# Banded distances: from differences and squares to products of queries parted on a grid

## The chip, the cores and the metric

The kernel runs on one core of one Trainium2 chip. The metric is the device time of one launch in microseconds. The core has five engines that work side by side and wait for each other by semaphores: TensorE (PE in the profile, its weight loads PEld), VectorE (DVE), ScalarE (ACT), GpSimd (POOL) and SyncE (SP), whose queue issues nearly all DMAs here. Data lies in SBUF and PSUM (128 partitions each) and in DRAM.

## The reference

Four layers run over x of shape (8, 1024, 128), each added to its input after a layer norm: full attention (16 heads), a feed-forward layer with weights of plus and minus one (called F1 below), a banded "top 32 of 64" attention, and the same feed-forward layer again (F2). The change touches only the banded attention:

```
q = relu(x @ encoder_query);  v = relu(x @ encoder_value)       # 8 heads of 16
metric = softplus(base_metric + 0.1 * mod)                      # from the mean of q, per batch, head, column
idx = clip(pos[:, None] - arange(64)[None, :], 0, T - 1)        # each row and the 63 before it
for h in range(8):
    diff = q_h[:, idx] - q_h[:, :, None]
    dist = sqrt((diff * diff * metric_h).sum(-1) + 1e-08)
    top 32 of 64 by smallest dist
    infl = exp(-topd) / (sum + 1e-08)
    context = sum(infl * v_h[rows chosen]) + gate * 0.1 * (qhat @ Hm)
    outs.append(q_h * context)
x = x + stack(outs) @ decoder
```

## The kernel before, in words

`full_attention` runs first over all eight batches and takes about half of the time. The other three layers follow together in `mixed_stages`. There each batch is described by generators of small operations, and a planner (`Issue`, from L63) merges all of them into one order before anything is issued. Each operation names its engine with an assumed length, what it needs and gives, and the buffers ("rings") that it takes and drops. The planner repeatedly takes the operation that can start earliest, the one due first among equals. It so sets the order on every engine and on SP's queue; at run time each engine goes through its own list in order and waits where it must. The assumed lengths, such as 2.6 for DVE's selection of a head pair, 0.2 for SP's two band stores and 2.5 for a DMA's landing, set the order only.

For each batch the steps are:

- `front` normalises x, turns it, projects the queries into `qT` (128 columns of all heads on the partitions, 1024 positions and a pad of 64 copies of the first) and computes the metric (DVE operations up to L1288, ACT's L1270).
- `differences` (L1330): for each half of 512 positions and each of 16 groups of four offsets, one operation subtracts the queries from the queries four times shifted, 128 x 2048 elements. Of the 32 such operations of a batch most go to POOL and three to DVE; in the first half of batch 0 the planner may use either (39 on DVE and 217 on POOL in all). The result, `sq`, has four buffers.
- `squares` (L1345) squares each of them on ACT; `distances` (L1362) multiplies by minus the metric and sums the 16 columns of each head on PE; `turned` (L1380, L1390, L1403) copies, transposes and copies, which gives `nd`, the negative squared distances with positions on the partitions: 128 positions x 4 tiles x 8 heads x 64 offsets for one half.
- `picks` (L1443, L1446) on DVE: for each tile of 128 positions and each head four rounds of "eight largest, then mark them". One planner operation does two heads; four make a tile, 64 tiles in all.
- `influence` (L1418) takes the root of a half; `selection` takes exp (L1466), keeps the chosen (L1478), sums (L1480) and divides (L1496) into `wr`. Two DMAs on SP write `wr` as bands into a DRAM buffer `skew` whose rows are shifted by one against each other (L1509); one DMA reads the buffer back straight, as `wb` (L1515). So a band becomes a 128 x 128 matrix per head.
- `contexts`: PE projects the values (L1599), transposes `wb` into `pw` (L1619), ACT copies it (`wT`, L1630), PE weighs the values (`pc`, L1646), DVE multiplies by the queries (`c`, L1659), PE decodes (`pd`, L1668) and DVE adds to x (L1673). `scaled` prepares the gated queries `qg`.
- The feed-forward units of F1 and F2 (L1023 to L1154) fill in between: POOL normalises, PE multiplies (L1070, L1105, L1132), ACT and DVE apply relu and split (`xh` L1059, `h` L1090), DVE adds (L1148).

`wb` has two buffers, `wT` one, `nd` three; a context therefore follows its tile's selection by some steps on every engine. What sets the end of a band is the way `wr` - `skew` - `wb` - `pw` - `wT` - `pc` - `c`.

Of the kernel before, what the change touches and what calls it, by code (L numbers as in the profile page):

```python
# [12 lines left out]
F32 = mybir.dt.float32  # L13
# [8 lines left out]
P = 128  # L22
# [31 lines left out]
SQ_BUFS = 4  # L54
# [8 lines left out]
class Issue:  # L63
# [24 lines left out]
    def next_slot(self, name):  # L88

        count, slots = self.rings[name]  # L90
        if name != self.ANY:
            return slots[count % len(slots)], count % len(slots)
        return min([(t, i) for i, t in enumerate(slots) if t is not None], default=(None, None))

    def begin(self, op):
# [6 lines left out]
        for name, _ in op.takes:  # L102
            t = self.next_slot(name)[0]
            if t is None:
                return []
            at = max(at, t + self.HOP)
# [180 lines left out]
def hybrid_kernel(ctx: ExitStack, tc: tile.TileContext, a: dict, out: bass.AP):  # L287
# [6 lines left out]
    ps_acc = ps_one = ident = None  # L294
# [14 lines left out]
    def load(pool, key, shape, view=None):  # L309
# [13 lines left out]
        "mn_b2": [P, 1], "base": [P, 1], "dec": [P, P], "nblk": [P, 4, SLOT], "pblk": [P, NH], "hm": [P, P],  # L323
# [8 lines left out]
    for t in range(NT):  # L332
        skew.append(dskew.tile([P, NH * P], F32, tag=f"skew{t}", name=f"skew{t}"))

# [601 lines left out]
    def mixed_stages():  # L936
        nonlocal ps_acc, ps_one
        with ExitStack() as st:
            ps_acc = st.enter_context(tc.tile_pool(name="ps_acc", bufs=2, space=PSUM))
            ps_one = st.enter_context(tc.tile_pool(name="ps_one", bufs=1, space=PSUM))  # L940
            def one(name):
                return bank(name, issue.slot)
            dlast = st.enter_context(tc.tile_pool(name="d_last", bufs=1, space=DRAM))
            pools = {
                n: st.enter_context(tc.tile_pool(name=f"mx{n}", bufs=n)) for n in (1, 2, 3, SQ_BUFS, 8)
# [3 lines left out]
            enc_q, enc_v, mn_w1, mn_b1, mn_w2, mn_b2, base, dec, nblk, pblk, hm = (  # L949
# [4 lines left out]
            for v in values:  # L954
                V.memset(v, 0.0)
            issue = Issue()
            for name, n in (
                ("acc", 2), ("one", 6), ("sq", SQ_BUFS), ("qT", 3), ("xnT", 3), ("qg", 2),
                ("nd", 3), ("e", 1), ("wk", 2), ("wr", 2), ("wb", 2), ("wT", 1), ("qv", 2), ("c", 2), ("nt", 2), ("gx", 1),
                ("fxn", 1), ("wxn", 1), ("xh", 2), ("h1", 1), ("h2", 1), ("statsQ", 2), ("statsF2", 2),  # L960
            ):
                issue.ring(name, n)
# [198 lines left out]
            def front(b, f):  # L1161
# [132 lines left out]
                def columns(e):  # L1294
                    f["mst"] = tile_(2, [P, 4, SLOT], "mst", f"mst_{b}")
                    A.activation(f["mst"], nblk, AF.Copy, scale=f["met"])

                yield op([("A", 0.35)], columns, needs=[(k, "met")], gives=[(k, "metric")])


            FOURS = [(blk, kk) for blk in range(4) for kk in range(4)]


            BESIDE = (0,), (0, 2)

            def differences(b, f):

                for half in range(2):
                    for n, (blk, kk) in enumerate(FOURS):
                        k = ("now", b, half)  # L1310
                        if n == BESIDE[half][0]:
                            def now(e, half=half):
                                f["now"] = one(f"now_{b}_{half}")
                                A.copy(f["now"], f["qT"][:, WIN + half * 512 : WIN + half * 512 + 512])

                            yield op([("A", 0.58)], now, needs=[(("Q", b), "qT")], gives=[k], takes=[("one", k)])

                        beside = n in BESIDE[half]
                        lanes = [("V", 2.35)] if beside else [("L", 2.35)] if b == 0 and half == 0 else [("G", 4.2)]

                        def go(e, half=half, blk=blk, kk=kk, beside=beside):
                            f["sq", half, blk, kk] = tile_(SQ_BUFS, [P, 4, 512], "sq", f"sq_{b}_{half}_{blk}_{kk}")
                            now = f["qT"][:, WIN + half * 512 : WIN + half * 512 + 512]
                            back = bass.AP(
                                now.tensor, now.offset - (16 * blk + kk + 12), [now.ap[0], [4, 4], [1, 512]]
                            )
                            if beside and e != "G":
                                now = f["now"]
                            lane = G if e == "G" else V
                            lane.tensor_tensor(  # L1330
                                f["sq", half, blk, kk], back, now.unsqueeze(1).to_broadcast([P, 4, 512]), ALU.subtract
                            )

                        yield op(
                            lanes, go, needs=[k if beside else (("Q", b), "qT")],
                            gives=[("d", b, half, blk, kk)], takes=[("sq", (b, half, blk, kk))],
                            drops=[("one", k)] if n == BESIDE[half][-1] else (),
                        )

            def squares(b, f):  # L1340
                for half in range(2):
                    for q in FOURS:
                        def go(e, key=("sq", half) + q):
                            s = f[key].rearrange("p a q -> p (a q)")
                            A.activation(s, s, AF.Square)  # L1345

                        yield op(
                            [("A", 1.95)], go, needs=[("d", b, half) + q], gives=[("s", b, half) + q]
                        )

            def distances(b, f):

                for half in range(2):
                    for blk in range(4):
                        for kk in range(4):
                            q = (half, blk, kk)

                            def go(e, half=half, blk=blk, kk=kk, q=q):
                                if kk == 0:
                                    f["psd"] = ps_acc.tile([P, 512], F32, tag="acc", name=f"psd_{b}_{half}_{blk}")  # L1360
                                for cg in range(4):
                                    PE.matmul(  # L1362
                                        f["psd"][cg * SLOT : (cg + 1) * SLOT, :], f["mst"][:, kk, :],
                                        f[("sq",) + q][:, 3 - cg, :], start=(kk == 0), stop=(kk == 3),
                                    )
                                f["psd", half, blk] = f["psd"]

                            yield op(
                                [("T", 1.05)], go, needs=[("s", b) + q, (("Q", b), "metric")],
                                gives=[("psd", b, half, blk)] if kk == 3 else (),  # L1370
                                takes=[("acc", (b, half, blk))] if kk == 0 else (), drops=[("sq", (b,) + q)],
                            )

            def turned(b, f):

                for half in range(2):
                    for blk in range(4):
                        def copy(e, half=half, blk=blk):
                            f["nt", half, blk] = tile_(2, [P, 512], "nt", f"nt_{b}_{half}_{blk}")
                            A.copy(f["nt", half, blk], f["psd", half, blk])  # L1380

                        yield op(
                            [("A", 0.58)], copy, needs=[("psd", b, half, blk)], gives=[("nt", b, half, blk)],
                            takes=[("nt", (b, half, blk))], drops=[("acc", (b, half, blk))],
                        )

                        def turn(e, half=half, blk=blk):
                            f["pt"] = one(f"pt_{b}_{half}_{blk}")
                            for i in range(4):
                                PE.transpose(  # L1390
                                    f["pt"][:, i * P : (i + 1) * P], f["nt", half, blk][:, i * P : (i + 1) * P], ident
                                )

                        yield op(
                            [("T", 0.6)], turn, needs=[("nt", b, half, blk)], gives=[("pt", b, half, blk)],
                            takes=[("one", ("pt", b, half, blk))] + ([("nd", (b, half))] if blk == 0 else []),
                            drops=[("nt", (b, half, blk))],
                        )

                        def put(e, half=half, blk=blk):  # L1400
                            if blk == 0:
                                f["nd", half] = tile_(3, [P, 4, NH, WIN], "nd", f"nd_{b}_{half}")
# [454 lines left out]
```

## Time and profile before

| what | value |
|---|---|
| median of 3 runs | 2678.91 us (2676.65 to 2679.77) |
| profiled execution, span | 2688.0 us |
| PE busy, whole span | 2449.8 us, 22084 matmul records |
| DVE busy | 2360.5 us, 8495 instructions |
| ACT busy | 2110.5 us, 2764 |
| POOL busy | 1361.2 us, 962 |
| DMA moved | 116.69 MB, mean 43 GB/s; queue of SP 19.2% of 16 DMA engines |
| HBM | 45.79 MB read, 27.26 MB written |
| first MAX8 of a selection starts | 1523.4 us |

The span runs from the first to the last instruction of one profiled execution and is 9.1 us above the median of the timed runs. Busy time of an engine counts a moment once, however many of its instructions overlap; instructions of DVE and PE are pipelined, so their single durations overlap by about a tenth of a microsecond and the sum of a group's durations is more than the time it takes. The mean of a group hides different shapes, so groups are taken by form.

### The profile page before, as it was taken

The page shows a single profiled execution, that of the slowest core. Times are in us where ns is not written, and L with a number is a line of the kernel's source. Part 1 is how long each engine was busy: PE and PEld are TensorE (multiplying, and loading weights), DVE is VectorE, ACT ScalarE, POOL GpSimd, SP SyncE. Part 2 cuts the span into 40 slices and gives each one's busy share as a digit, 9 for nine tenths or more (in the row PEclk, how much of TensorE's full clock was granted, in tenths as well). Part 3 has the DMA queues.
Part 4 walks back from the last instruction along what each step waited for, and adds up shares of the span by engine and source line. Part 5 has one row for each costly group of instructions (what it writes and reads, how often), then busy time and mean ns, then how long its engine had stood idle before and what let it go on. Part 6 is the DMA issues. An engine that isn't in the chain of part 4 may idle for free.

```text
span 2688.0 us, 59925 instructions
## 1 busy us (share of the span) xinstructions
PE 2449.8 (91%) x22084; PEld 1387.5 (52%) x22084; DVE 2360.5 (88%) x8495; ACT 2110.5 (79%) x2764; POOL 1361.2 (51%) x962
## 2 busy tenths in 40 slices
PE   5999999999999999999999786998988898989677
PEld 2444444444444444444448363665656575746266
DVE  6999899898998989989954989999889999998985
ACT  1888788887888878888884878888888888888752
POOL 3202404114041140410203589999998999999931
PEclk6999999999999999999999888999989999989797
DMA  3312232121221212122100021222111222122221
GB/s 76 71 30 58 48 72 48 24 51 23 42 41 32 45 28 42 37 37 41 34 8 11 1 48 48 50 54 49 46 37 50 50 54 50 41 52 48 56 56 44
DMA packets 149693, 116.69 MB, mean 43 GB/s; under 512 B 96984, under 2 KB 127640, under 8 KB 149400
## 3 DMA queue, kind: packets, MB, share of 16 engines
q1 hardware_dynamic: 146216, 111.75, 19.2%
q8 instruction: 174, 2.85, 0.5%
q10 hardware_dynamic: 3184, 1.12, 0.2%
q14 instruction: 119, 0.97, 0.1%
HBM read 45.79 MB, written 27.26 MB: 27 GB/s over the span
## 4 chain that ended last, share of the span: by engine, by line
PE 62%; DVE 12%; POOL 10%; ACT 8%; DMA 5%; issue 2%; SPq 0%; ACTq 0%; POOLq 0%; DVEq 0%
PE acc L741 19%; PE ps L708 15%; PE pm L659 11%; POOL sq L1330 8%; DVE wk L1446 4%; PE psd L1362 3%; DVE m L1443 3%; ACT sq L1345 2%; DMA wb<-skew 2%; DMA skew<-wr 2%; DVE mx L663 1%; ACT e L720 1%; PE pw L1619 1%; PE pp L512 1%; POOL wxn L1023 1%
## 5 line engine op out<-in xcount | busy, mean ns | idle before, releaser
L663 DVE TENSOR_REDUCE mx<-pm 128x2 f32<-128x1024 f32 x1024 | 1202.3, 1217 | 137.2 <-PE pm L659 130.5
L1330 POOL TENSOR_TENSOR sq<-qT 128x2048 f32<-128x2048 f32 x217 | 896.4, 4162 | 7.8 <-PE psd L1362 7.5
L720 ACT ACTIVATE e<-ps 128x1024 f32<-128x1024 f32 x671 | 687.5, 1025 | 174.3 <-PE ps L708 153.4
L708 PE MATMUL ps<-q,k 64*128 64x512 f32 x2048 | 580.7, 443 | 13.2 <-ACT e L727 7.3
L741 PE MATMUL acc<-e,v 128*32 128x256 f32 x8192 | 591.1, 389 | 0.0
L1345 ACT ACTIVATE sq<-sq 128x2048 f32<-128x2048 f32 x256 | 488.4, 1916 | 50.6 <-POOL sq L1330 43.0
L659 PE MATMUL pm<-k,q 64*128 64x512 f32 x2048 | 490.3, 450 | 17.6 <-DMA q<-qs 9.0
L683 POOL TENSOR_TENSOR negm<-mm,negm 128x16 fp32r<-128x16 f32 x64 | 14.9, 233 | 818.9 <-ACT negm L682 818.9
L727 ACT ACTIVATE e<-ps 128x512 f32<-128x512 f32 x706 | 419.3, 594 | 5.0 <-PE ps L708 4.9
L708 PEld LDWEIGHTS ps<-q,k 64*128 64x128 f32 x2048 | 256.5, 185 | 262.5 <-ACT e L720 146.7
L1362 PE MATMUL psd<-sq,mst 128*32 128x512 f32 x2048 | 294.1, 653 | 75.5 <-ACT sq L1345 73.2
L741 PEld LDWEIGHTS acc<-e,v 128*32 128x32 f32 x8192 | 195.0, 109 | 289.5 <-issue 213.7
L659 PEld LDWEIGHTS pm<-k,q 64*128 64x128 f32 x2048 | 215.2, 187 | 188.8 <-DVE mx L663 85.4
L1446 DVE MATCH_REPLACE8 wk<-m,wk 128x64 f32<-128x64 f32 x1536 | 309.9, 210 | 0.0
L1443 DVE MAX8 m<-wk 128x8 f32<-128x64 f32 x1536 | 267.2, 217 | 0.0
L1619 PE MATMUL pw<-ident,wb 128*128 128x128 f32 x512 | 90.0, 309 | 56.8 <-DMA wb<-skew 49.3
L1446 DVE MATCH_VALUE_LOAD wk<-m,wk 128x8 f32 x1536 | 125.0, 81 | 0.0
L1619 PEld LDWEIGHTS pw<-ident,wb 128*128 128x128 f32 x512 | 65.8, 157 | 100.4 <-issue 53.6
L1362 PEld LDWEIGHTS psd<-sq,mst 128*32 128x32 f32 x2048 | 42.8, 111 | 135.5 <-ACT sq L1345 105.9
L1630 ACT COPY wT<-pw 128x512 f32<-128x512 f32 x128 | 74.2, 585 | 48.5 <-PE pw L1619 48.3
L1446 DVE MATCH_REPLACE8 wk<-m,nd 128x64 f32<-128x64 f32 x512 | 103.3, 210 | 0.0
L1443 DVE MAX8 m<-nd 128x8 f32<-128x64 f32 x512 | 87.5, 213 | 10.9 <-ACT nd L1403 10.9
(2211 smaller groups left out, 3739.8 us busy)
## 6 DMA issues: line engine op xcount, KB each, us to landing
wb<-skew SPq DMA_DIRECT2D x64, 512.0 KB
k<-ks SPq DMA_DIRECT2D x256, 64.0 KB
skew<-wr SPq DMA_DIRECT2D x128, 128.0 KB
q<-qs SPq DMA_DIRECT2D x252, 64.0 KB
x<-in_x SPq DMA_DIRECT2D x8, 512.0 KB
q<-dm SPq DMA_DIRECT2D x256, 8.0 KB
skew<-zeros SPq DMA_DIRECT2D x8, 512.0 KB
out_x<-x SPq DMA_DIRECT2D x32, 128.0 KB
```

What stands on the lines that cost most here:

```text
L659: PE.matmul(ps[:, j * 512 : j * 512 + 512], q[r, t * P : (t + 1) * P], k[r, kh * 512 : kh * 512 + 512], start=True, stop=True,)
L663: V.tensor_reduce(D["mx", n][:, kh, t, 2 * pair : 2 * pair + 2], ps.rearrange("p (j k) -> p j k", j=2), AX.X, ALU.max, negate=True,)
L708: PE.matmul(ps, sides[n % 3]["k", pair][r, c * P : (c + 1) * P], sides[n % 3]["q", pair][r, half * 512 : half * 512 + 512], start=True, st ...
L720: A.activation(e, ps, AF.Exp, scale=SCALE)
L727: A.activation(es[u], ps, AF.Exp, scale=SCALE)
L741: PE.matmul(acc[h * SLOT : (h + 1) * SLOT, part * 256 : part * 256 + 256], v[:, c, (g * 4 + h) * (HD_A + 1) : (g * 4 + h) * (HD_A + 1) + S ...
L1330: lane.tensor_tensor(f["sq", half, blk, kk], back, now.unsqueeze(1).to_broadcast([P, 4, 512]), ALU.subtract)
L1345: A.activation(s, s, AF.Square)
L1362: PE.matmul(f["psd"][cg * SLOT : (cg + 1) * SLOT, :], f["mst"][:, kk, :], f[("sq",) + q][:, 3 - cg, :], start=(kk == 0), stop=(kk == 3),)
L1443: V.max(m8, wk_[:, h, :] if n else f["nd", half][:, t % 4, h, :])
L1446: V.match_replace(out=wk_[:, h, :], in_to_replace=m8, in_values=wk_[:, h, :] if n else f["nd", half][:, t % 4, h, :], imm_value=SELECTED,)
L1619: PE.transpose(g["pw", hh][:, i * P : (i + 1) * P], f["wb", t][:, hh * 4 + i, :], ident)
```

## The change

The squared distance is computed as a product instead of by subtraction. With p = q times the square root of the metric, -d2/2 between a query row i and a key row j is p_i.p_j - |p_i|2/2 - |p_j|2/2. Here p is parted into h, rounded on a coarse grid (by adding and subtracting a large number `big`), and l = p - h, and the products of the parts are summed. Each head then has 52 rows: for the queries h, h, l and the norms, for the keys h, l, p and the norms, with rows of ones against the norms.

What happens now for each batch, besides the old steps that stay:

- `front` loses `columns` and gains `weighed`, `bound`, `roots` and `refined`: the bound `big` (a small product on PE and a root on ACT) and the root of the metric, refined by one step on DVE.
- `rows` for each half (512 positions and the 64 before them): ACT rounds (`h`), POOL scales (`p`) and takes off the bound, ACT squares `h`, POOL forms `l`, p + h and (p + h) l; three DMAs store `h`, `p`, `l` (each 128 x 576) in DRAM; twelve DMAs fetch them, sixteen rows at a time, into `queries` and `keys` (two heads of a pair on partitions 0 and 64, four pairs beside each other); PE sums the norms, ACT copies them, one DMA stores and four fetch them.
- `grams` for each tile: 16 products of 52 rows, 64 queries by 128 keys, into two PSUM banks, one product in each quarter of the array; two ACT copies, with the columns in reverse, into `dt`; one DMA stores the tile in `flat`; two DMAs fetch the bands from rows shifted by one, straight into `nd`; POOL clamps at zero.
- `picks` of a tile wait for that tile's band only, no longer for the half. `nd` has two buffers in place of three; the sums `acc` give their two PSUM banks to the common ring, which has eight. The heads stand in another order in `nd`, which `weigh` follows.
- The scratch space for DMAs issued by POOL is set to 1024.

Deleted: `differences`, `squares`, `distances`, `turned` and the constant `nblk`. Full attention is unchanged.

```diff
-                def columns(e):
-                    f["mst"] = tile_(2, [P, 4, SLOT], "mst", f"mst_{b}")
-                    A.activation(f["mst"], nblk, AF.Copy, scale=f["met"])
...
+                def weighed(e):
+                    f["mw"] = tile_(2, [P, 1], "mw", f"mw_{b}")
+                    V.tensor_scalar(f["mw"], f["met"], squared[0], None, ALU.mult)
...
+                    PE.matmul(f["psb"][:, 0:1], blk, f["mw"], start=True, stop=True)
...
+                    A.activation(f["root"], f["met"], AF.Sqrt)
+                    A.activation(f["big"], f["psb"][:, 0:1], AF.Sqrt, scale=GRID)
...
+                    V.tensor_scalar(f["sm"], f["root"], 1e-18, None, ALU.max)
+                    V.reciprocal(f["sm"], f["sm"])
+                    V.tensor_scalar(f["sm"], f["sm"], f["met"], f["root"], ALU.mult, ALU.add)
+                    V.tensor_scalar(f["sm"], f["sm"], 0.5, None, ALU.mult)
...
+            ROWS = ((0, "h", 2), (0, "h", 18), (1, "h", 2), (1, "p", 34), (0, "l", 34), (1, "l", 18))
+            NORMS = ((0, 1), (50, 51))
+
+            def rows(b, f):
...
+                        A.activation(g["h"], q(), AF.Identity, bias=f["big"], scale=f["sm"])
...
+                        G.tensor_scalar(g["p"], q(), f["sm"], None, ALU.mult)
+                        G.tensor_scalar(g["h"], g["h"], f["big"], None, ALU.subtract)
...
+                        [("A", 0.7)], lambda e, g=g: A.activation(g["2"], g["h"], AF.Square), needs=[(k, "h")],
...
+                        [("G", 1.25)], lambda e, g=g: G.tensor_tensor(g["l"], g["p"], g["h"], ALU.subtract),
...
+                        [("G", 1.25)], lambda e, g=g: G.tensor_tensor(g["w"], g["p"], g["h"], ALU.add),
...
+                        [("G", 1.25)], lambda e, g=g: G.tensor_tensor(g["w"], g["w"], g["l"], ALU.mult),
...
+                        S.dma_start(parted[half][name], g[name])
...
+                    def send(e, side, name, at, half=half):
+                        to, skip = ((queries, WIN), (keys, 0))[side]
+                        src = parted[half][name].rearrange("(g a d) t -> a d g t", g=NH // 2, a=2)
+                        for par in range(2):
+                            r = par * 64 + at
+                            S.dma_start(to[half][r : r + HD, :, :], src[par, :, :, skip:])
...
+            def grams(b, f):
...
+                        for g in range(NH // 2):
+                            for par, a2 in ((0, 0), (1, 1), (0, 1), (1, 0)):
+                                r = slice(par * 64, par * 64 + 52)
+                                c = c0 + a2 * 64
+                                PE.matmul(
+                                    ps[par][a2 * 64 : a2 * 64 + 64, g * P : (g + 1) * P],
+                                    queries[half][r, g, c : c + 64], keys[half][r, g, c : c + P], start=True, stop=True,
+                                )
...
+                            v = f["dt", t][:, par * 4 : par * 4 + 4, P - 1 : P]
+                            A.copy(
+                                bass.AP(v.tensor, v.offset, [list(v.ap[0]), list(v.ap[1]), [-1, P]]),
+                                f["pg", t][par].rearrange("p (g c) -> p g c", c=P),
                             )
...
+                    def store(e, t=t):
+                        S.dma_start(flat[t].rearrange("p (h c) -> p h c", c=P), f["dt", t])
...
+                            band = bass.AP(
+                                s.tensor, s.offset + a2 * 64 * NH * P + WIN - 1,
+                                [[NH * P - 1, 64], [P, NH], [1, WIN]],
                             )
...
+                            S.dma_start(f["nd", half][a2 * 64 : a2 * 64 + 64, t % 4], band)
...
+                        G.tensor_scalar(v, v, 0.0, None, ALU.min)
...
-                            AF.Sqrt, bias=tiny_t, scale=-1.0,
+                            AF.Sqrt, bias=tiny_t, scale=-2.0,
...
-                        [("V", 2.6)], marks(hh), needs=[("nd", b, half)],
+                        [("V", 2.6)], marks(hh), needs=[("nd", b, t)],
...
-                    ("differences", differences, 0.0, 1.0),
-                    ("squares", squares, 0.0, 1.0), ("distances", distances, 0.0, 1.0), ("turned", turned, 0.1, 1.05),
+                    ("rows", rows, -0.15, 0.35), ("grams", grams, 0.1, 1.0),
...
-    nc = bacc.Bacc("TRN2", target_bir_lowering=False, num_devices=1)
+    nc = bacc.Bacc("TRN2", target_bir_lowering=False, num_devices=1, dynamic_dma_scratch_size=1024)
```

## The prediction

> **What bounds the kernel now.** I read the page's forty slices first, to place the change, then busy time by window, the costliest groups, the waits, and the timelines of DVE and SP.
>
> ```profile
> DVE  6999899898998989989954989999889999998985
> POOL 3202404114041140410203589999998999999931
> ...
> 1406.00:2688.00 1282.00, 1086.07 (x9541) 751.44 (x9537) 1130.40 (x7300) 987.49 (x1212) 1042.90 (x524) 0.92 0.18 45
> 1469.00:1523.00 54.00, 43.20 (x320) 24.88 (x319) 51.23 (x66) 48.70 (x48) 15.30 (x12) 0.94 0.00 1
> 1523.00:2580.00 1057.00, 905.49 (x8045) 607.01 (x8043) 983.48 (x6687) 873.52 (x1048) 998.65 (x452) 0.92 0.20 48
> 2580.00:2688.00 108.00, 78.96 (x710) 70.67 (x709) 74.34 (x484) 36.75 (x66) 9.07 (x25) 0.85 0.22 55
> ```
>
> Window rows give the stretch, its length, then busy us of PE, weight loads, DVE, ACT and POOL, the granted clock, DMA share and GB/s. The first 21 slices are full attention, which the change leaves alone; the mixed stages fill the last 1282 us. In their middle stretch (1057 us) POOL is busy 999 and DVE 983: two engines at the bound together, so taking work off POOL alone leaves DVE's 983.
>
> ```profile
> L1330 POOL TENSOR_TENSOR sq<-qT 128x2048 f32<-128x2048 f32 x217 | 896.4, 4162 | 7.8 <-PE psd L1362 7.5 <-issue 0.3
> L1345 ACT ACTIVATE sq<-sq 128x2048 f32<-128x2048 f32 x256 | 488.4, 1916 | 50.6 <-POOL sq L1330 43.0 <-DVE sq L1330 6.7
> L1330 DVE TENSOR_TENSOR sq<-qT,now 128x2048 f32<-128x2048 f32 x24 | 54.5, 2274 | 0.0
> L1330 DVE TENSOR_TENSOR sq<-qT 128x2048 f32<-128x2048 f32 x15 | 33.7, 2284 | 0.0
> ```
>
> The change deletes all four groups. POOL loses 896 us and ACT 488, but DVE only 54.5 + 33.7 = 88 (39 subtractions). What DVE keeps is selection: one head pair of L1443 and L1446 runs on the timeline from 2580.94 to 2583.54, while POOL is idle, and from 2101.64 to 2104.24, while POOL is busy: 2.6 us both times. So POOL's relief does not speed it up; 64 tiles x 4 pairs x 2.6 = 666 us stay.
>
> **Up to the first selection.** The first MAX8 starts at 1523.4. Of DVE's 39 subtractions 18 lie before it, between 1469.7 and 1520. The new way to the first tile of distances is a chain of latencies: the queries are ready at 1468.0; the metric ends at 1481.9 now and some 2 us earlier without the three subtractions that DVE puts before it. Then: scale and bound, 3.8 us (five DVE operations of 0.2, a table load of 1.28, two ACT operations of 0.25, a product and hand-overs about 1); rounding on ACT 0.7 (0.60 for 512 columns); two POOL operations, 1.8 (a 128x1024 copy takes 1.3); a store and its landing, 3.8; twelve row fetches on SP at 0.63, 7.5; norms stored, landed and fetched, 0.6 + 3.4 + 2.5 + 3.4; products 1.3 and two copies of 0.59; store 0.33 + 3.6; two band fetches 1.25 + 3.4; clamp 0.8. From 1480 that ends at 1519.4, with hand-overs near 1521. So the lead-in is as long as before, and 18 of DVE's 39 subtractions buy nothing. Bounds: 10 us either way.
>
> **DVE from there to the end.** Busy now: 983.5 + 74.3 = 1057.8. Minus the 21 subtractions in it, 2.22 from start to start, 46.6. Plus five one-column operations for seven batches at 0.245 (L1285's step), 8.6. Minus 6 for feed-forward work that the order of the changed kernel puts ahead of the first selection. Sum 1013. That is the floor for what follows.
>
> **Idle on top.** Now 1164.6 - 1057.8 = 107: 34 after 2580 and 73 before. The last twenty DVE instructions stand in the same order in both kernels, so the 34 stays. Of the 73, waits for `nd` (9.1) go, since the order fetches bands some three tiles, 45 us, ahead; the other 64 come from waits such as `s<-qT`, `xh`, `h` and `c`. Without the last I keep 25, between 15 (ACT falls from 987 to near 540: minus 576 for squares and copies, plus 128 copies of 0.59 and 50 of small work) and 49 (all but `nd`, `c` and `x`'s 4.6).
>
> The loop through DRAM is different, because SP is one queue in order:
>
> ```profile
> 2193.59 0.69 DVE L1496 TENSOR_TENSOR wr<-pe,den 128x512 f32<-128x512 f32 x1
> ...
> 2194.30 1.25 SPq L1509 DMA_DIRECT2D skew<-wr  x2
> 2199.22 0.33 SPq L1515 DMA_DIRECT2D wb<-skew  x1
> ...
> 2017.07 3.44 DMA wb<-skew
> ...
> 1104.58 5.02 SPq L627 DMA_DIRECT2D q<-qs  x8
> ...
> DVE c L1659 <- PE pc L1646: 10.0, 12, 1.9
> SPq L1515 <- DMA skew<-wr: 214.0, 80, 4.2
> ```
>
> From the end of `wr` to the earliest `c`: 4.95 to the issue of the fetch, 3.6 for its landing, 3 for transposes, copies and `pc`: 11.8 us. DVE has other work between the two: summing its order by these durations, 16 to 30 us in a middle batch now (hence only 10.0 us of waits), 18.8, 11.5, 13.5, 17.3, 13.2, 18.4, 14.8, 14.2 for the eight tiles in the changed order. There SP also has, per tile, a flat store, a wait and two band fetches (0.33 + 3.4 + 1.25 = 5.0), and per half three stores, twelve row fetches, a norm store and four norm fetches. Queued behind a waiting band fetch are the next `skew` store, so `wb`, PE's `pw` and what PE holds after it. A store that meets such a round trip waits half of it, 2.5 us. Chain 14.3: the tiles fall short by 2.8, 0.8, 1.1 and 0.1, 4.8 a batch, 38 in all. With no delay: 0.3 a batch, 2. With a full 5.0: 16.8 a batch, 134. I take 38, the middle delay; both ends stay for the range.
>
> **What the other engines take on.** PE loses `psd` (8 records in 0.96, 256 times: 246) and `pt` (64 x 0.6 = 38). Its products, 16 of 52x64 by 128 per tile in four quadrants, are nearest to `pc`'s 16 of 64 columns in four column groups, 0.65 us: doubled 1.3, 83 us in all; with no overlap 16 x 0.3 (half of `psv`'s 0.61 for two) = 4.8, 307. Norms add 35. PE ends at 1086 - 284 + 118 = 920, hidden under DVE; in the bad case 1144, and not hidden. POOL: 147 of old small work, 16 halves of five operations of about 1.1 (L1330's 1.9 to 2.2 ns a column) and 64 clamps of 0.5 to 1.8, some 300; hidden, but a clamp waiting for its band holds back POOL's normalisations. DMA: about 91 MB more beside 58 now, so the share of 0.18 becomes near 0.5.
>
> From the trace, the granted clock was 0.77 in 2486 to 2554, where PE was busy 44 of 68 us, and 1.00 in 2150 to 2218 with 65 of 68. [...] By the rows, at the 0.85 of the last window (PE busy 79 of 108), 920 becomes 996, still under DVE's 1013 plus idle; I take these.
>
> SP's issue time is not small here: 46 DMAs per half at 0.33 to 0.63 (the eight `q<-qs` above took 5.02 us), so I keep the 38. [...]
>
> **Sum.** 1521 + 1013 + 25 + 38 + 34 = 2631 beside the profiled span of 2688.0. The median of the runs, 2678.9, lies 9.1 below that span: 2622, 2.1% less.
>
> **Rivals.**
> DVE alone, nothing late: lead-in 1515, 1013, idle 15 + 2, tail 30, less 9: 2566. For it: `c` waits only 10.0 us now. Against: the distances shrank to 11.5.
>
> SP becomes the bound (the slower side). Per batch by the rows: 8 x (1.25 + 0.33) for the old pair, 8 x (0.33 + 1.25) for the new, 32 row and norm fetches at 0.63, eight stores at 0.4, four outputs at 0.45, about 51 of issue; 16 waits of 3.4 and four of 2, 62; minus some 15 where the order puts other DMAs inside a wait: 98 of DVE's 127. It decides once a batch takes (2688 - 1521 - 34) / 8 = 142, that is when landings take 1.7 times as long under 2.5 times the traffic. With landings doubled: 98 + 62 = 160, 8 x 160 + 1555 - 9 = 2826; at 1.8 times 148 and 2727, which I take. Against: DMA share would be 0.5, not 1.
>
> PE becomes the bound, the quadrants not overlapping: 1144 of work where 1086 filled 1282 now; about as before, 2690. Against: `pc`'s 32 records in 0.65.
>
> **How the numbers follow.** Forecast 0.52 (own range 2580 to 2680); DVE alone 0.17; SP 0.20; PE 0.11. The predicted time is the forecast's. For 8 in 10 the range goes down to 2560 for most of the second case and up to 2715 for PE's and the near edge of SP's. No change is within 0.2% (5.4 us, about what a measurement of this kernel can tell). Faster: 0.50 + 0.17 + 0.01 + 0.04 = 0.72; same 0.04; slower 0.24.
>
> **What would show it.** First selection at 1510 to 1530; DVE busy near 1013 after it and over 90%; POOL below 350 and ACT below 600 in the mixed stages; products near 1.3 us a tile; `c` waiting for `pc` some 40 us. SP's wait for `flat` or `skew` near 6 us, and DVE idle over 150, would show SP's case; `pc` or `h` waits with PE over 95%, PE's. I am wrong if the first selection is late by more than 20 us, or DVE's own work is not 1013.

## The result and the profile after

The changed kernel takes 2787.98 us (median of 4 runs, 2779.37 to 2793.27) where the kernel before takes 2677.78 us (4 runs): a ratio of 1.0409, 95% interval 1.0388 to 1.0429. The forecast was 2622 us and its range ended at 2715.

First the slices of the page after, as they were read before, and the window rows of its mixed stages (the stretch, its length, busy us of PE, weight loads, DVE, ACT and POOL, granted clock, DMA share, GB/s).

```profile
DVE  6999898998989989899723778796878788887895
POOL 3203213141140411402024313223231323223111
...
1530.00:2680.00 1150.00, 778.64 (x7952) 684.27 (x7951) 940.03 (x6672) 493.06 (x862) 308.11 (x360) 0.79 0.48 120
2680.00:2782.00 102.00, 65.30 (x615) 59.35 (x613) 73.54 (x501) 30.45 (x55) 9.25 (x25) 0.84 0.18 54
```

POOL and ACT are relieved as planned (999 of 1057 us to 308 of 1150, and 874 to 493, in the middle), but DVE's digits fall too, from 9 to 7 and 8. No engine is full any more: DVE stands idle for 210 of the 1150 us. A table makes the end from three parts: the start of the first selection, DVE's busy time from there, and the rest of the span, in which DVE waits. They are taken from the trace's DVE instructions.

| kernel | first MAX8 | DVE busy from there | DVE idle from there | span |
|---|---|---|---|---|
| before | 1523.4 | 1057.9 | 106.6 | 2688.0 |
| predicted | 1521 | 1013 | 97 | 2631 |
| after | 1532.4 | 1013.6 | 236.2 | 2782.2 |

DVE's own work came out to the microsecond, with some luck: other orders of the same instructions, below, have 999.0 to 1013.6. Of the 151 us between forecast and profile, 139 are idle time. The waits from 1406 us on show what it waits for (who waits, line, for whom; us in all, times, longest). First the two of the kernel before that matter:

```profile
PE pw L1619 <- DMA wb<-skew: 49.3, 18, 6.8
ACT wT L1630 <- PE pw L1619: 48.3, 29, 8.9
```

and those of the kernel after:

```profile
POOL nd L1534 <- DMA nd<-flat: 374.4, 53, 17.4
ACT wT L1758 <- PE pw L1747: 303.6, 97, 11.5
PE pw L1747 <- DMA wb<-skew: 286.0, 57, 12.6
DVE c L1787 <- PE pc L1774: 52.6, 18, 9.5
...
DVE pe L1606 <- ACT pe L1594: 36.2, 19, 5.3
...
DVE den L1618 <- ACT den L1613: 26.6, 13, 3.5
...
DVE m L1571 <- POOL nd L1534: 8.7, 1, 8.7
```

The bands (`nd`) are there in time: POOL waits for them, but DVE's selection waits for POOL once, 8.7 us. PE waits nearly six times as long for `wb` as before, ACT as long again behind PE, and DVE behind ACT. Summed over all units, DVE's waits from 1530 us on are 52.6 for `c`, 47.4 for `xh`, 36.2 for `pe`, 32.5 for `h`, 26.6 for `den` from ACT and 21.0 for `x`. Four of these six wait for ACT, an engine that is busy 43% of the time.

One place in the timeline of the kernel after shows how an idle engine comes to be late (start, us, engine; in brackets the idle time before). The `wr` in question ends on DVE at 1761.83.

```profile
1763.43 1.27 SPq L1637 DMA_DIRECT2D skew<-wr  x2
1768.15 0.87 POOL L1034 TENSOR_SCALAR fxn_('F2', 0)_2_21876<-x,rstd_('F2', 0)_20039,shift_('F2', 0)_20040 128x128 f32<-128x128 f32 x2 [2.56 <-PE psT_('F2', 0)_1_21866 L1057]
1771.33 0.34 SPq L1643 DMA_DIRECT2D wb<-skew  x1
...
1775.97 1.94 PE L1747 MATMUL pw<-ident,wb 128*128 128x128 f32 x8 [7.93 <-DMA wb<-skew]
1777.70 0.63 PE L1057 MATMUL psT_('F2', 0)_2_21890<-ident,fxn_('F2', 0)_2_21876 128*128 128x128 f32 x2
...
1777.10 0.59 ACT L1758 COPY wT<-pw 128x512 f32<-128x512 f32 x1 [8.38 <-PE pw L1747]
1778.43 0.38 ACT L1065 CAST xh_('F2', 0)_2_21942<-psT_('F2', 0)_2_21890 128x256 fp32r<-128x256 f32 x1
...
1778.84 0.42 DVE L1070 TENSOR_TENSOR xh_('F2', 0)_2_21943<-psT_('F2', 0)_2_21890,xh_('F2', 0)_2_21942 128x256 fp32r<-128x256 f32 x1 [6.70 <-ACT xh_('F2', 0)_2_21942 L1065]
```

PE's list has `pw` next and `wb` has not landed, so PE stands for 7.93 us. Behind `pw` in the same list is a feed-forward transpose (`psT`), whose input POOL had ready at 1769.02; it starts at 1777.70. ACT stands 8.38 us before `wT`, with the cast of that unit behind it, and DVE waits 6.70 us for ACT. The unit that DVE waits for has nothing to do with the band that is late: it merely stands behind it in a queue.

Not every long wait is of this kind alone. Before a similar one, of 8.11 us, at 2106.12, PE waits 7.65 us for `wb` too, but there the input of `psT` was late itself, because POOL's normalisation stood behind a clamp that waited for its band:

```profile
2100.51 1.48 POOL L1534 TENSOR_SCALAR nd<-nd 128x512 f32<-128x512 f32 x1 [5.64 <-DMA nd<-flat]
2101.98 0.88 POOL L1034 TENSOR_SCALAR fxn_('F2', 2)_2_26376<-x,rstd_('F2', 2)_24319,shift_('F2', 2)_24320 128x128 f32<-128x128 f32 x2
```

How much each of the two is worth is a question for the experiments.

Over tiles 4 to 59 (means, from the starts and ends of these instructions), the way from the end of `wr` to `c` took 17.4 us after and 20.3 before, so the loop itself did not get slower. DVE's other work inside it fell from 18.8 us to 14.3.

### The profile page after: what moved, and what is told of

It is laid out like the page before. It is cut to its first block, busy times and chain, and to the rows that moved or that the text cites. A ratio compares the mean times of both kernels' runs of the same rounds, so it can differ in the third digit from the quotient of the medians.

```text
span 2782.2 us, 60297 instructions
## 1 busy us (share of the span) xinstructions
PE 2315.6 (83%) x21974; PEld 1472.7 (53%) x21974; DVE 2284.9 (82%) x8498; ACT 1706.6 (61%) x2577; POOL 688.9 (25%) x896
## 5 line engine op out<-in xcount | busy, mean ns | idle before, releaser
L1747 PE MATMUL pw<-ident,wb 128*128 128x128 f32 x512 | 110.7, 370 | 314.2 <-DMA wb<-skew 286.0
L1747 PEld LDWEIGHTS pw<-ident,wb 128*128 128x128 f32 x512 | 83.6, 192 | 327.5 <-issue 266.7
L1534 POOL TENSOR_SCALAR nd<-nd 128x512 f32<-128x512 f32 x64 | 95.2, 1487 | 444.9 <-DMA nd<-flat 374.4
L1484 PE MATMUL pg<-keys,queries 52*64 52x128 f32 x2048 | 93.0, 332 | 8.9 <-DMA keys<-part_n 4.8
L1499 ACT COPY dt<-pg 128x512 f32<-128x512 f32 x128 | 70.0, 586 | 46.4 <-PE pg L1484 39.9
L1484 PEld LDWEIGHTS pg<-keys,queries 52*64 52x64 f32 x2048 | 73.3, 166 | 21.8 <-issue 10.6
```

Of the source, the lines that this page charges most:

```text
L1484: PE.matmul(ps[par][a2 * 64 : a2 * 64 + 64, g * P : (g + 1) * P], queries[half][r, g, c : c + 64], keys[half][r, g, c : c + P], start=True ...
L1534: G.tensor_scalar(v, v, 0.0, None, ALU.min)
L1747: PE.transpose(g["pw", hh][:, i * P : (i + 1) * P], f["wb", t][:, hh * 4 + i, :], ident)
```

## The experiments

Two theories were set against each other. O: the order is at fault. The planner assumes 0.2 + 2.5 + 0.1 + 2.5 us for the store, its landing, the fetch and its landing, where the trace has 1.39, 3.67 and then some 4 us until PE starts. It therefore puts `pw` and `wT` too early into the lists of PE and ACT. Q: SP's queue and the DMA traffic of rows and bands are at fault. Beside them: C, the lower clock of TensorE (0.79 where it was 0.92), and B, late bands. The kernel before ran with each group, at 2675.6 to 2677.5 us.

**e_loop: tell the planner the loop's lengths.** No instruction changes, only their order.

```diff
-                self.done[n] = end + (self.TAIL[e] if e else 0.0)
+                self.done[n] = end + (self.TAIL[e] if e else 0.0) + (2.0 if n[0] == "wb" or n[-1] == "skew" else 0.0)
...
-                yield op([("S", 0.2)], store, needs=[(k, "w")], gives=[(k, "skew")], drops=[("wr", (b, t))])
+                yield op([("S", 1.25)], store, needs=[(k, "w")], gives=[(k, "skew")], drops=[("wr", (b, t))])
...
-                yield op([("S", 0.1)], fetch, needs=[(k, "skew")], gives=[("wb", b, t)], takes=[("wb", (b, t))])
+                yield op([("S", 0.33)], fetch, needs=[(k, "skew")], gives=[("wb", b, t)], takes=[("wb", (b, t))])
```

> Only the assumed lengths of the loop wr - skew - wb change: 1.25 and 0.33 us of issue in place of 0.2 and 0.1, and 4.5 us in place of 2.5 for each of the two landings. Theory O (the written order: PE and ACT reach pw and wT before wb has landed, and all that is queued behind them waits): the waits of PE pw for wb (286 us) and of ACT wT for pw (304 us) fall by at least half, DVE's idle time after the first selection falls by 70 to 120 of its 240 us, and the time from 2788 to 2670 to 2720. Theory Q (SP's queue or the DMA traffic is what is slow): work in the loop is no faster for being planned later, 2775 to 2800. Theory C (TensorE's lower clock, 0.79 in place of 0.92): less than 30 us gained, 2760 to 2790.

2657.45 us, ratio 0.9932 to the kernel before (0.9908 to 0.9956): 131 us less than the kernel after, more than theory O's range held, and faster than the kernel before. Its waits:

```profile
ACT wT L1758 <- PE pw L1747: 91.0, 66, 6.7
PE pw L1747 <- DMA wb<-skew: 87.6, 25, 9.3
DVE c L1787 <- PE pc L1774: 27.1, 17, 4.2
...
DVE pe L1606 <- ACT pe L1594: 7.3, 6, 1.8
```

Both long waits fall to less than a third and DVE's idle time from 236.2 to 108.9 us, while POOL still waits 357.8 us for the bands. In the same loop SP's part became longer, not shorter (4.37 us from the store to the fetch in place of 3.67), and the clock in the middle is 0.82. Neither Q nor C allows for that gain.

**e_bands: tell it the other loop's lengths.** The same edit for `flat` and `nd`.

```diff
+                self.done[n] = end + (self.TAIL[e] if e else 0.0) + (2.0 if n[-1] in ("flat", "nd") and n[0][0] == "D" else 0.0)
```

> Only the assumed lengths of the loop dt - flat - nd change: 0.33 and 1.25 us of issue in place of 0.1 and 0.2, and 4.5 us in place of 2.5 for both landings. Theory O: nothing much, 2770 to 2805, since DVE waits for nd only 9 us; PE's wait for wb stays above 230 us. Rival B (the bands come late and hold back POOL, and with it the feed-forward units): 50 us gained or more, 2740 or less.

2769.62 us (ratio 1.0345, 1.0318 to 1.0372): 18 us less than after, just below O's range, where B asked for 50 or more. PE still waits 274.6 us for `wb`. B is not the main cause. POOL's wait for the bands fell from 374.4 to 270.8 us only, so what the rest of it costs stays open.

**e_before_loop: the same lengths for the kernel before.** The edit is e_loop's.

> The kernel before with the same lengths told for the loop wr - skew - wb as in e_loop. Theory O: there DVE's own work covered the loop in most tiles (18.8 us of it between wr and c, and only 49 us of PE's waiting for wb), so at most a quarter of e_loop's gain: 2645 to 2680 from 2678. If the gain were as large as in e_loop (2600 or less), the wrong lengths would have cost both kernels the same and could not explain the difference.

2663.03 us (ratio 0.9946, 0.9925 to 0.9967). The wrong lengths cost the kernel before 14 us and the kernel after 131.

**e_no_rows and e_loop_no_rows: leave the rows out**, first under the order of the kernel after, then under e_loop's.

```diff
-                        for par in range(2):
+                        for par in range(2 if b == 0 else 0):
...
+                        if b == 0:
+                            S.dma_start(parted[half][name], g[name])
```

> From batch 1 on the eight stores and thirty-two fetches of a batch's rows and norms are left out (each product is then formed of batch 0's rows), the planned order stays as it is. Theory Q: SP's queue loses 38 us of issue in 142 and more than a third of the traffic, so 80 us or more are gained, 2710 or less. Theory O: the order and the loop's latency decide; the loop waits a little less behind other DMAs, 10 to 45 us gained, 2743 to 2778. Theory C: 2780 to 2795.

> e_loop and e_no_rows together. Without the loop's lengths told, leaving out the rows was worth 75 us (2788 to 2712). Theory O: that was the loop's own latency shortened by about 1 us per tile under an order with no slack; with slack in the order it is worth little, 0 to 30 us, 2627 to 2657. Theory Q (rows and bands load SP and the DMA engines, a cost of its own): again 50 us or more, 2607 or less.

e_no_rows: 2712.52 us (ratio 1.0136, 1.0106 to 1.0166), 75 us less than after: more than O expected, less than Q did. e_loop_no_rows: 2607.21 us (ratio 0.9736, 0.9719 to 0.9754), still 50 us less than e_loop, where O expected at most 30. So O is not all of it: the rows have a cost of their own. DVE's idle time goes 236.2 to 163.2 in the first pair and 108.9 to 65.0 in the second, its busy time stays within 4 us in both. In the loop of the second pair, the store of `skew` is issued 0.11 us after `wr` in place of 0.74, and the fetch of `wb` 3.61 us after the store in place of 4.37.

**e_loop_small: issues or bytes?** Every row DMA is still issued, from batch 1 on with 16 columns.

```diff
-                            S.dma_start(to[half][r : r + HD, :, :], src[par, :, :, skip:])
+                            n = 512 if b == 0 else 16
+                            n += (WIN - skip) * (b == 0)
+                            S.dma_start(to[half][r : r + HD, :, :n], src[par, :, :, skip : skip + n])
```

> e_loop with every row and norm DMA still issued, but from batch 1 on of 16 columns in place of 512 or 576 (80 in the stores), so that the rest of a product's rows is batch 0's. e_loop_no_rows was 50 us faster than e_loop. If the rows cost by their issues on SP's queue, ahead of the skew stores and the fetches of wb (there 0.74 us from wr to the store's issue and 4.37 us from there to the fetch, against 0.11 and 3.61 without rows), the time stays at 2645 to 2660. If they cost by their bytes (share of the DMA engines 0.53 against 0.36), it falls to 2605 to 2620. In between: both.

2612.56 us (ratio 0.9762, 0.9739 to 0.9786). With all of the issues and almost none of the bytes it stands 5 us from e_loop_no_rows, and the two intervals overlap; 45 of the 50 us are bytes. The window rows of e_loop and of e_loop_small show the DMA share and the rate that went with them:

```profile
1530.00:2560.00 1030.00, 755.45 (x7946) 653.77 (x7944) 944.94 (x6769) 489.72 (x849) 311.52 (x372) 0.82 0.53 134
```
```profile
1530.00:2560.00 1030.00, 781.01 (x8168) 677.61 (x8164) 984.66 (x7067) 504.79 (x875) 315.57 (x385) 0.82 0.37 103
```

Share 0.53 against 0.37, at the same clock, and 40 us more of DVE's work done in the same stretch. The issues did not get shorter with the bytes: a DMA of rows or norms took 0.48 us of SP's time in e_loop and 0.47 in e_loop_small (means of 1700 to 2500 us). What got shorter is the loop around them: the store of `skew` is issued 0.31 us after `wr` in place of 0.74, and the fetch of `wb` follows its store after 3.87 us in place of 4.37. That the higher DMA share (0.53 against 0.37) is what stretched these transfers is an estimate from the two windows; no run shows it apart from the bytes.

**e_act: move the rows to ACT's queue** (with the planner told as in e_all2 below).

```diff
-                            [("S", 1.3)], lambda e, a=(side, name, at), send=send: send(e, *a), needs=[(k, "kept", name)],
+                            [("A", 0.85)], lambda e, a=(side, name, at), send=send: send(e, *a), needs=[(k, "kept", name)],
...
-                            S.dma_start(to[half][r : r + HD, :, :], src[par, :, :, skip:])
+                            A.dma_start(to[half][r : r + HD, :, :], src[par, :, :, skip:])
```

> As e_all2, but the stores and fetches of rows and norms are issued by ACT, and planned there with 0.41 and 0.85 us of its time. If SP's order is what the rows cost, the stores of skew no longer stand behind them (0.1 us in place of 0.5 to 0.7) and 10 to 40 us are gained on e_all2. If their bytes cost, nothing is gained, and ACT's 100 us of issue and its waits for landings may cost 0 to 40 us.

2680.19 us (ratio 1.0018, 1.0005 to 1.0032), 66 us more than e_all2. The store of `skew` does come sooner (0.17 us after `wr` in place of 0.41), but ACT now stands until row and norm fetches land (13.8 us in five waits before `split_h`, 12.5 in one before `dt` and 12.4 in one before `pe`), and DVE's wait for ACT's `pe` grows from 2.3 to 35.1 us. The loss is larger than expected; that it is ACT's issues and not the planner's new lengths was not separated.

**b_light and b_light_loop: the kernel before, relieved without rows or bands.** What made its order loose?

```diff
-                        lanes = [("V", 2.35)] if beside else [("L", 2.35)] if b == 0 and half == 0 else [("G", 4.2)]
+                        lanes = [("V", 2.35)] if beside else [("L", 2.35)] if b == 0 and half == 0 else [("G", 1.1)]
...
+                            lane, n = (G, 1) if e == "G" else (V, 4)
...
-                            s = f[key].rearrange("p a q -> p (a q)")
+                            s = f[key][:, 0, :]
```

> The kernel before, with POOL and ACT relieved and nothing else: of every POOL subtraction and of every square only the first of the four offsets is computed (its square is used four times), with 1.1 and 0.6 us told to the planner in place of 4.2 and 1.95. No new rows, no bands, no new DMA; DVE keeps all its work. Theory O: the saturated POOL was what kept DVE's other work between wr and c long; relieved, the planner draws the loop tight on its wrong lengths, PE's waits for wb rise from 49 us to over 150 and the time hardly falls or even rises: 2660 to 2710. If relief alone were worth what DVE's own work allows (1523 + 1058 + 25 + 34 - 9), the time would be 2615 to 2640 and the loss would lie in the rows and bands (theory Q).

> b_light with the loop's lengths told to the planner as in e_loop. Theory O: PE's waits for wb fall again below 100 us and the time by 40 to 70 against b_light, to 2600 to 2650. Theory Q: as b_light within 15 us.

b_light: 2688.19 us (ratio 1.0047, 1.0031 to 1.0063). With POOL busy 356 of 1030 us in the middle and ACT 578, the kernel is no faster; DVE's idle time is 105.5 us, as before. PE's waits for `wb` rose to 71 us only, less than half of what was expected, but ACT's behind PE rose as in the kernel after, and new waits of DVE for ACT's `pe` (23.5 us) stand where others went:

```profile
ACT wT L1631 <- PE pw L1620: 122.8, 72, 7.8
PE pw L1620 <- DMA wb<-skew: 71.1, 20, 9.0
DVE pe L1479 <- ACT pe L1467: 23.5, 18, 2.8
```

The loop shrank to 17.1 us with 15.9 us of DVE's work in it, from 20.3 and 18.8. Told the lengths, b_light_loop takes 2638.45 us (ratio 0.9857, 0.9842 to 0.9871), 50 us less, with 59.9 us of DVE idle. So relief of POOL and ACT tightens this order by itself, without any of the new DMAs, and here it brought time only with the loop's true lengths.

**e_all and e_all2: tell it everything.** Hand-over 0.3, the POOL operations by their rows, `flat` 0.33, `nd` 1.25 and the loop's issues; landings 3.5 in e_all; 3.0, and 4.0 in the loop, in e_all2.

```diff
-    HOP = 0.1
+    HOP = 0.3
-    TAIL = {"V": 0.0, "A": 0.0, "G": 0.1, "T": 0.2, "S": 2.5, "L": 0.0}
+    TAIL = {"V": 0.0, "A": 0.0, "G": 0.1, "T": 0.2, "S": 3.0, "L": 0.0}
...
-                        [("G", 0.6)], clamp, needs=[(k, "nd")],
+                        [("G", 1.5)], clamp, needs=[(k, "nd")],
```

> The planner is told all lengths of the steps that the change touches, from the changed kernel's rows: skew 1.25, wb 0.33, flat 0.33, nd 1.25, landings 3.5 for all DMAs, clamp 1.5, the POOL operations of the split 3.5 and 1.42, normalisations 0.9 and 1.8, and a hand-over between engines of 0.3 in place of 0.1. Theory O: PE's waits for wb stay below 100 us, those of DVE for ACT fall further (pe, xh, h), 10 to 50 us below e_loop: 2607 to 2647. If the loop was all, the same as e_loop within 8 us.

> e_all with 3.0 us for a landing in place of 3.5 and 4.0 us for the two landings of the loop, which the rows of e_loop show as the slowest (4.37 us from the skew store's issue to that of the fetch). Expected a few us below e_all: 2615 to 2640, DVE's waits below 95 us.

e_all: 2637.61 us (ratio 0.9848, 0.9831 to 0.9865), though PE's waits for `wb` grew to 131.0 us. e_all2: 2614.29 us (ratio 0.9775, 0.9752 to 0.9799), a little below its range and 174 us below the kernel after with the same instructions. It is the fastest kernel of this study that computes everything. The 23 us between e_all and e_all2, for half a microsecond in the assumed landings, show what a new order alone can shift: e_loop's 131 are far above that, the 14 of e_before_loop and the 18 of e_bands are within it. Its windows show DVE at 95% in the middle stretch:

```profile
1531.00:2512.00 981.00, 731.98 (x7818) 633.76 (x7807) 929.84 (x6714) 475.61 (x841) 306.21 (x360) 0.83 0.56 141
2512.00:2611.00 99.00, 76.12 (x717) 69.93 (x715) 69.33 (x437) 33.76 (x62) 9.53 (x26) 0.88 0.21 60
```

The parts of the span, as in the first table:

| kernel | first MAX8 | DVE busy | DVE idle | span |
|---|---|---|---|---|
| after | 1532.4 | 1013.6 | 236.2 | 2782.2 |
| e_bands | 1537.3 | 1008.6 | 226.6 | 2772.6 |
| e_no_rows | 1535.5 | 1012.9 | 163.2 | 2711.5 |
| e_loop | 1537.4 | 1009.7 | 108.9 | 2656.0 |
| e_loop_no_rows | 1536.6 | 1005.8 | 65.0 | 2607.4 |
| e_loop_small | 1534.5 | 1007.8 | 70.3 | 2612.5 |
| e_all | 1535.9 | 999.5 | 100.3 | 2635.8 |
| e_all2 | 1533.0 | 999.0 | 78.8 | 2610.9 |
| e_act | 1534.7 | 1003.4 | 139.3 | 2677.3 |
| before | 1523.4 | 1057.9 | 106.6 | 2688.0 |
| e_before_loop | 1524.5 | 1055.4 | 81.5 | 2661.4 |
| b_light | 1519.0 | 1059.7 | 105.5 | 2684.2 |
| b_light_loop | 1519.4 | 1054.7 | 59.9 | 2634.0 |

Most of the difference between the variants of one kernel is in the idle column.

## Why the prediction was wrong, point by point

- **First selection, 1521 with 10 us either way.** 1532.4: 11 late, just past the bound. In the trace the metric ended at 1485.8 where the chain started from 1480, and scale and bound took 6.1 us in place of 3.8; that is 8 of the 11. POOL's two operations took 3.5 in place of 1.8.
- **DVE from there, 1013.** 1013.6. Right, and POOL's relief did not make DVE's operations faster (MAX8 on `wk` 217 ns in the mean before, 215 after). The last few microseconds are luck, since the order alone moves this number by up to 15.
- **Idle, 25.** This is the first step that failed. It held that waits such as `xh` and `h` would shrink because ACT's load falls from 987 to 540. ACT's load fell to 581, and DVE's waits for ACT grew from 47 us to 143 (now for `xh`, `pe`, `h` and `den`), since ACT was late behind PE, not busy. With the next step, 25 + 38 = 63 us were kept for idle time before the tail; it was 207.
- **The loop, 38.** The second, and the same error: the chain was set against DVE's work for each tile, rightly found short of it, and only the shortfall at `c` was paid for. That wait itself was near the forecast (52.6 us against some 40). What stands behind the waiting instruction was listed for SP's queue and named for PE ("what PE holds after it"), but not priced for PE and for ACT. SP's delay was over-priced: 0.48 us on average in place of 2.5. The end of the loop was under-priced: from the first `pw` to `c` 7.5 us in place of 3. The trace before could have told, since there the same way took 8.6, and the whole way from `wr` to `c` 20.3 in place of 11.8 (whose terms add up to 11.55).
- **16 to 30 us of DVE's work in the loop before, 11.5 to 18.8 after.** This was the sign to follow. The prediction saw it and did not ask why a planner should leave less. Its rows held the answer: an assumed 0.2 against 1.25 for the store, and 2.5 against 3.4 to 3.6 for the landings.
- **Tail, 34.** Right in the main: in the last 108 us of the span DVE stood idle for 29.
- **PE.** Products: 93 us for 64 tiles, 1.45 each, against the estimates of 1.3 with overlap of the quadrants and 4.8 without. The records overlap: at 1632.59 four of a tile's 32 start within 0.02 us of each other and the next four 0.11 us later, each 0.27 us long. PE is busy 951 us in the mixed stages, between the forecast's 920 and 996, and not the bound: the PE rival fell.
- **POOL and ACT.** POOL 371 us where "below 350" was said (a clamp takes 1.49 us, the split's operations 1.42 to 1.73 in place of 1.1); ACT 581, as said. That a waiting clamp holds back normalisations is seen at 2101.98 (above); e_bands cut POOL's wait for the bands from 374 to 271 us, for 18 us of time, and nothing cut the rest.
- **SP as the bound.** It fell. Of its two signs, DVE idle over 150 came (236), but SP waited 2.2 us for `skew` and 2.7 for `flat` on average from 1530 to 2680, not near 6. The wait from the store's issue to that of the fetch grew from 3.52 to 3.67 us on average, not by 1.7 times, and the issues of the row and norm DMAs (40 in a batch) are worth about 5 us of the whole time under e_loop's order. In e_loop_small the issues stayed and 45 us went with the bytes; in e_act, with the row DMAs on ACT's queue, `wb` still followed `skew` after 4.37 us, as against 4.29 in e_all2.
- **DMA share near 0.5.** 0.48. The prediction took that for harmless. Under e_loop's order, which leaves more slack in the loop (16.9 us of DVE's work in it against 14.3), leaving out the rows gains 50 us; under the order of the kernel after 75.
- **What made the time.** Telling the planner the loop is worth 131 of the 166 us between forecast and result, with no instruction changed; leaving out the rows' bytes as well brings the kernel to 2607 to 2613. Fully told, with all of its work, it reaches 2614, so the gain that was forecast lay in the change, but not in the order it was given. That 2614 comes near 2622 does not confirm the sum: DVE's work is 14 us less there, its idle time 18 less and the first selection 12 later.

The half-speed clock was not separated. In the place shown below it began during such a wait, and PE's matmuls of 256 columns then followed each other by 0.21 us in place of 0.12, so that a part of what the order costs may come by way of it.

## What to carry to other kernels

Where a planner writes the order of in-order queues, a change of load is also a change of order: set its assumed lengths against the trace's rows for every step that comes to matter, and walk the new order with the measured ones. A wait is priced with all that stands behind it in the waiting engine's queue, and behind the engine that waits for that one; an engine with a low load can be the one that is late (ACT here, busy 43% of the middle stretch). Slack that a saturated engine gave can go when the engine is relieved (with POOL and ACT relieved in b_light, 15.9 us of DVE's work in the loop in place of 18.8), and then small things can have a price, such as the rows' bytes here, 45 us under e_loop's order.

## What the runs showed of the hardware

In the kernel after, TensorE's granted clock fell from 1.00 to 0.50 during PE's wait before 2102.46 us (at 2098.1, 3.3 us after PE's last product) and stayed down after it:

```profile
2094.00:2102.40 8.40, 0.81 (x19) 0.40 (x10) 4.01 (x31) 2.23 (x4) 2.76 (x3) 0.75 0.68 169
2102.40:2108.30 5.90, 5.84 (x28) 5.87 (x29) 2.14 (x8) 1.68 (x4) 1.33 (x4) 0.50 0.05 15
2108.60:2113.00 4.40, 4.40 (x40) 4.38 (x39) 3.17 (x22) 2.23 (x6) 0.00 (x0) 1.00 0.29 119
```

For 5.9 us after a wait of 7.65 us PE runs without a gap at a granted clock of 0.50, and then at 1.00; matmuls of 256 columns follow each other by 0.21 us first and by 0.12 then. What makes the clock fall and rise was not shown. From 1406 us on the granted clock is at half for 209 us before, 548 after, 430 in e_loop and 365 in e_all2.

SP's issue of a pair of `skew` stores took 1.28 us in the median tile and 2.00 at 2090.99, behind row fetches and a `flat` store of 1.00. That the traffic stretched it is not shown: the mean is 1.39 us in the kernel after and 1.33 in e_no_rows.
